# The first sequence's tokens at the head of the queue, rows of weights behind them, and a new timetable for a two-layer kernel

## The chip, the core and the metric

The kernel runs on one core of a Trainium2 chip. Five engines each work through a queue of their own in order: TensorE (PE) multiplies matrices, VectorE (DVE) does elementwise work and scans, ScalarE (ACT) does functions such as exp and SiLU, GpSimd (POOL) gathers, scatters and adds, SyncE (SP) issues transfers (DMA). Semaphores order the engines among each other. The metric is the device time of one execution in microseconds.

## The reference

Eight sequences of 1024 tokens of width 128 go through two layers. Each half of a layer adds its result to x after a layer norm:

```python
x = L0_attn_x                                       # (8, 1024, 128)
x = x + L0_attn(layernorm(x))   # state = state * decay + k v^T, out = q state, per head, then o_w
x = x + L0_ffn(layernorm(x))    # 8 experts (hidden 352), the best 2 of each token: W2(silu(W1 x) * W3 x)
x = x + L1_attn(layernorm(x))   # conv3, silu, selective scan with 16 states, gate, Wout
x = x + L1_ffn(layernorm(x))    # 8 experts (hidden 128), best 2, and two shared experts
```

## The kernel before

Each of the 32 halves (8 sequences, 4 kinds) is a generator that records operations with an engine, what they read and write, and a time wanted (`sched.at`). Nothing is issued at recording. `Schedule.run` then walks through all operations, estimates when each could start, and emits them; the order in which it emits an engine's operations is that engine's queue on the chip. The estimates do not reach the chip: only the order does.

Three things steer the order. `TIMES` has a row for each sequence: a time for the load of its x, and for each half the time of its first, second and last step, with the steps between spaced evenly. An operation with a lower time goes first among those that can start. `START` has the times of loads that belong to no sequence: `START[0]` for `w_rows` (the experts' weights of layer 0 copied in DRAM into one row of 1088 numbers for each expert and partition: W1T, W3T, a block of zeros, three parts of W2T), `START[1]` to `START[4]` for the zeroing of the four buffers `xd` into which tokens are scattered, `START[5]` for `f_rows` (the experts' weights of layer 1). Four numbers set the choice in `run`: `NEAR` (how much later than the earliest possible start an operation may start and still be chosen by its time), `AHEAD` and `STAY` (how far ACT keeps to operations of the function table that it holds before it loads the other), and `TABLE` (the estimate of a load).

```python
soon = max(min(start for start, _ in able), clock[e]) + NEAR
_, start, o = min((o.at, start, o) for start, o in able if start <= soon)
```

The loads of `w_rows`, `xd`, `f_rows` and x are made with `hold=True`, by `load` (L453): they don't start before their time in `run`'s estimate. All plain transfers go out on SP's queue; the constants (L264, L282, L294, L343 to L346) go out on ACT's, ahead of ACT's first computing.

The halves work like this. Layer 0's attention (`l0_attn`): layer norm (`normal`: statistics on DVE L478, Ln and Exp on ACT, scaling on ACT L494), transposes on PE (L508), projections (L462), v written to DRAM (`v_rows`) and read back as eight tiles `kv` in which each head's row is repeated; for each tile a product, a scan (L757) and a product on DVE, and in two groups of four the products with `o_rep` on PE (L647), added to x by DVE. Layer 0's experts (`l0_ffn`): routing on DVE (with the counts on PE, L583 and L584), a scatter of tokens to `xd` by POOL (16 indirect transfers, L813), then 23 blocks of 128 tokens. For each: the weights of its expert fetched (`we`, L870, three buffers), the tokens `xg` loaded and transposed in pairs (L856), the first product on PE (L925), SiLU on ACT, a product on DVE (`h`), the second product on PE (L904, recorded one block late), a scaling on ACT (L879), a store to `yd`; at the end a gather and add by POOL (L832, L421). Layer 1's attention (`l1_attn`): for each of 16 states exp on ACT, two products on PE that spread a row (L462, from `eye3b`), a product, a scan (L1025) and a product on DVE, and an add on POOL. Layer 1's experts (`l1_ffn`) are like layer 0's in pairs of blocks (L1129, L1110), but for the last sequence, where all experts run densely (`l1_ffn_dense`). Five buffers hold x, so up to five sequences are in work.

Of the kernel before, what the change touches and what calls it, by code (L numbers as in the profile page):

```python
# [50 lines left out]

PE, DVE, ACT, POOL, SP = ENGINES = "PE", "DVE", "ACT", "POOL", "SP"
HOP = 0.1
NEAR = 0.000
TABLE = 1.3
AHEAD = 139.9
STAY = 808.88


FREE = "wide", "acc", "row", "tile64", "xg", "xgT", "h", "ysb"  # L60


TIMES = (
    (0.00, (818.90, 1322.01, 2108.68), (3522.25, 4588.46, 4795.69), (4797.48, 4983.83, 4992.58), (5030.92, 5042.54, 5223.89)),
    (67.14, (3166.92, 3983.92, 4510.55), (4699.80, 4856.34, 4927.28), (4997.29, 5212.77, 5286.76), (5404.61, 5424.23, 5749.45)),
    (109.51, (4187.39, 4691.07, 4889.13), (4901.24, 4939.80, 5127.57), (5251.15, 5545.42, 5789.16), (5810.49, 5812.68, 6004.33)),
    (120.45, (4793.10, 4906.69, 4971.56), (5082.33, 5219.46, 5502.99), (5722.81, 6084.57, 6157.33), (6169.97, 6173.73, 6677.38)),
    (236.36, (5055.60, 5281.59, 5442.24), (5660.84, 5668.06, 5941.03), (5949.96, 6234.77, 6774.15), (6878.69, 6968.14, 7691.04)),
    (479.09, (5388.91, 5651.37, 5789.26), (5874.46, 5982.25, 6396.69), (6719.00, 7084.49, 7401.94), (7715.74, 7724.19, 8166.75)),
    (809.61, (5867.01, 6125.06, 6365.51), (6586.67, 6776.94, 7240.89), (7646.86, 8055.63, 8649.36), (8989.08, 9535.91, 10103.79)),  # L70
    (976.52, (6289.32, 6518.36, 6888.36), (7137.22, 7366.30, 7806.48), (8156.41, 9711.12, 9827.21), (9899.41, 10070.31, 10173.34)),
)

START = -2834.48, 135.59, 64.01, 104.85, 731.91, 32.55


class Buf:
# [20 lines left out]
class Schedule:  # L98
# [45 lines left out]
    def run(self):  # L144
# [3 lines left out]
        for _ in range(len(self.ops)):  # L148
            best = None
            for e in ENGINES:  # L150
# [15 lines left out]
                if same:  # L166
# [5 lines left out]
                        or c[1].table == table  # L172
                        or clock[e] - c[0] > STAY
                        or c[1].at[0] + AHEAD < min(same)
                    ]
                soon = max(min(start for start, _ in able), clock[e]) + NEAR
                _, start, o = min((o.at, start, o) for start, o in able if start <= soon)
# [33 lines left out]
def preln_two_layer_kernel(ctx: ExitStack, tc: tile.TileContext, a: dict, out: bass.AP):  # L211
# [239 lines left out]
    def load(out_, in_, kb, r, w, hold=False):  # L451
        op(
            SP, 0.45, lambda: nc.sync.dma_start(out_(), in_()), r, w, land=2.3 + kb / 300.0,  # L453
            hold=hold,
        )
# [229 lines left out]
    w_rows_b, f_rows_b = Buf(None, w_rows), Buf(None, f_rows)  # L685
    sched.at = START[0]
    for j, name in enumerate(("W1T", "W3T")):
# [17 lines left out]
    for i, v in enumerate(xd_b):  # L705
        sched.at = START[1 + i]
        load(
            lambda v=v: v.f.rearrange("(b p) d -> p b d", p=P),
            lambda: zrow.unsqueeze(1).to_broadcast([P, NBLK, XW]), 1483, [], [v], hold=True,
        )  # L710
    sched.at = START[5]
    for j, name in enumerate(("w1T", "w3T", "w2T")):
# [533 lines left out]
```

## Time and profile before

| | us |
|---|---|
| median of 3 runs (2008.73 to 2019.97) | 2010.96 |
| the profiled execution | 2010.04 |
| its span, first to last instruction | 2007.9 |
| DVE busy | 1445.7 (72%) |
| PE busy | 1383.3 (69%) |
| ACT busy, of it 254.0 in 198 loads of a function table | 1000.1 (50%) |
| POOL busy | 891.4 (44%) |

The mean granted TensorE clock was 0.826. A line of the timeline has the start and the length in us, the engine (SPq and ACTq: the sequencer issues a transfer), the line of the kernel, the operation, out<-in, and in brackets how long the engine had been idle and what ended that. A line of the waits has who waited for whom: us in total, times, the longest. A line of the groups ends with busy us, mean ns of one, and the idle time just before.

### The profile page before, as it was taken

Reading aid. Unit: us, or ns where it says so; the run is one execution under the profiler, and the core shown is the slowest. Engines: PE = TensorE matmul, PEld = TensorE weight load, DVE = VectorE, ACT = ScalarE, POOL = GpSimd, SP = SyncE. Lnnn points to the kernel's source line nnn. Section 1 sums busy time; section 2 is a strip of 40 time slices with the busy share of each in tenths; the row PEclk is TensorE's granted clock in tenths of the full one; section 3 lists DMA queues with packets and bytes.
Section 4 is the critical chain, followed back from the end, with each engine's and each line's share of the span. In section 5 each row is a group of like instructions: output and inputs, shape, how many; then the busy total and the mean of one; then the engine's idle time right before and its main releaser. Section 6 shows DMA issues by size and latency. Waiting matters only on the chain. (4 is left out here: it accounts for less than half of the span.)

```text
span 2007.9 us, 24885 instructions
## 1 busy us (share of the span) xinstructions
PE 1383.3 (69%) x7693; PEld 1060.4 (53%) x7693; DVE 1445.7 (72%) x2117; ACT 1000.1 (50%) x1657; POOL 891.4 (44%) x662
## 2 busy tenths in 40 slices
PE   0557787775875678667766686675776788566588
PEld 0335676663554566446655465455665576343364
DVE  0687557767847997699766876679857745789955
ACT  1323443743865475455745447363544576583341
POOL 0003205246135851484643554438635626646613
PEclk9778988877988789769978697786888798796679
DMA  5685668443345458445537463454454566232232
GB/s 161 134 159 157 192 185 232 132 123 112 112 137 156 116 159 203 118 143 144 168 111 200 110 183 121 125 152 126 135 154 143 159 199 190 80 99 59 74 108 58
DMA packets 215740, 282.54 MB, mean 141 GB/s; under 512 B 24248, under 2 KB 173112, under 8 KB 215608
## 3 DMA queue, kind: packets, MB, share of 16 engines
q1 hardware_dynamic: 194504, 247.81, 44.0%
q0 software_dynamic: 15360, 31.61, 5.3%
q10 hardware_dynamic: 5744, 1.54, 0.3%
q8 instruction: 61, 1.00, 0.2%
q14 instruction: 71, 0.58, 0.1%
HBM read 223.62 MB, written 63.15 MB: 143 GB/s over the span
## 5 line engine op out<-in xcount | busy, mean ns | idle before, releaser
L421 POOL TENSOR_TENSOR y<-y,st 128x1024 f32<-128x1024 f32 x120 | 293.1, 2443 | 296.4 <-DVE st L421 257.8
L925 PE MATMUL wide<-xgT,we 128*128 128x128 f32 x2208 | 328.6, 308 | 74.6 <-DVE st L1025 21.7
L832 POOL DMA_INDIRECT tmp<-yd,at x240 | 260.3, 1085 | 260.5 <-issue 59.1
L925 PEld LDWEIGHTS wide<-xgT,we 128*128 128x128 f32 x2208 | 308.1, 221 | 103.6 <-issue 29.4
L1025 DVE TENSOR_TENSOR_SCAN st<-da,wide 128x1024 f32<-128x1024 f32 x128 | 292.4, 2284 | 8.1 <-POOL y L421 0.3
L462 PE MATMUL wide<-term,eye3b 96*128 96x512 bf16 x512 | 181.4, 453 | 128.5 <-DVE st L1025 72.5
L393 ACT ACT_TABLE_LOAD x198 | 254.0, 1283 | 16.1 <-DMA gbias<-in_gate_bias_dram 12.7
L813 POOL DMA_INDIRECT xd<-xw,at x120 | 124.5, 1038 | 222.3 <-DVE at L634 162.7
L904 PE MATMUL acc<-we,h 128*128 128x128 f32 x1104 | 173.4, 298 | 70.4 <-DVE h L421 34.1
L446 ACT ACTIVATE h<-wide 128x384 f32<-128x384 f32 x184 | 89.4, 490 | 256.0 <-PE wide L925 158.6
L879 ACT ACTIVATE ysb<-acc,xg 128x128 f32<-128x128 f32 x345 | 116.7, 363 | 184.2 <-PE acc L904 70.4
L904 PEld LDWEIGHTS acc<-we,h 128*128 128x128 f32 x1104 | 153.6, 208 | 98.2 <-DVE h L421 31.0
L421 DVE TENSOR_TENSOR wide<-dtx,wide 128x1024 f32<-128x1024 f32 x128 | 156.4, 1223 | 58.3 <-remote 43.2
L446 ACT ACTIVATE da<-dt,a_mat 128x1024 f32<-128x1024 f32 x128 | 145.2, 1146 | 101.3 <-DVE st L1025 65.6
L647 PE MATMUL acc<-o_rep,kv 128*128 128x128 f32 x1024 | 150.0, 313 | 50.6 <-DVE kv L421 34.7
L421 DVE TENSOR_TENSOR h<-h,wide 128x384 f32<-128x384 f32 x184 | 99.2, 546 | 108.3 <-ACT h L446 85.4
L647 PEld LDWEIGHTS acc<-o_rep,kv 128*128 128x128 f32 x1024 | 144.4, 227 | 58.6 <-DVE kv L421 37.4
L421 DVE TENSOR_TENSOR st<-st,wide 128x1024 f32<-128x1024 f32 x120 | 146.2, 1218 | 34.9 <-PE wide L462 13.1
L757 DVE TENSOR_TENSOR_SCAN kv<-lam,kv 128x1024 f32<-128x1024 f32 x64 | 152.3, 2380 | 1.4
L462 PEld LDWEIGHTS <-eye3b 96*128 96x128 bf16 x512 | 57.3, 112 | 177.7 <-issue 165.8
L1129 PE MATMUL acc<-xgT,fe 128*128 128x128 f32 x644 | 119.9, 340 | 39.5 <-DMA fe<-f_rows 11.5
L792 POOL COPY tmp<-xw 128x1024 f32<-128x1024 f32 x15 | 19.5, 1297 | 280.4 <-ACT xw L494 208.3
(149 smaller groups left out, 2292.1 us busy)
## 6 DMA issues: line engine op xcount, KB each, us to landing
we<-w_rows SPq DMA_DIRECT2D x184, 544.0 KB
kv<-v_rows SPq DMA_DIRECT2D x64, 512.0 KB
fe<-f_rows SPq DMA_DIRECT2D x169, 192.0 KB
xg<-xd SPq DMA_DIRECT2D x165, 129.0 KB
yd<-ysb SPq DMA_DIRECT2D x165, 128.0 KB
xd<-zrow SPq DMA_DIRECT2D x4, 1483.5 KB
x<-in_x_dram SPq DMA_DIRECT2D x8, 512.0 KB
v_rows<-tmp SPq DMA_DIRECT2D x8, 512.0 KB
```

Of the source, the lines that this page charges most:

```text
L393: nc.scalar.add_instruction(mybir.InstLoadActFuncSet(name=nc.get_next_instruction_name(), act_func_set_id=tables[table], ins=[], outs=[]))
L421: op(eng, us, lambda: e.tensor_tensor(out_(), in0(), in1(), alu), r, w)
L446: op(ACT, act_us(n), lambda: nc.scalar.activation(out_(), in_(), func, **kw), r, w, table)
L462: nc.tensor.matmul(dst.f[:m, ts(s, HALF)], lhsT(), rhs()[:, ts(s, HALF)], start=True, stop=True)
L647: nc.tensor.matmul(v3(po, 4, P)[:, i, :], h.f[:, ts(4 * q + i, P)], w(), start=(j == 0), stop=(j == len(parts) - 1),)
L757: lambda kv=kv: nc.vector.tensor_tensor_scan(kv.f, lam.f, kv.f, 0.0, ALU.mult, ALU.add),
L813: lambda k=k, c=c: nc.gpsimd.indirect_dma_start(out=views[k * NC + c], out_offset=bass.IndirectOffsetOnAxis(ap=v3(at, TOPK, NC)[:, k, c : ...
L832: lambda k=k, c=c, g=g: nc.gpsimd.indirect_dma_start(out=v3(g, NC, P)[:, c, :], out_offset=None, in_=yd[i], in_offset=bass.IndirectOffsetO ...
L904: nc.tensor.matmul(py.f[:, :P], v3(h, 3, P)[:, j, :], we.f[:, c0 : c0 + P], start=(j == 0), stop=(j == 2),)
L925: nc.tensor.matmul(p4[:, m, j, :], we.f[:, c0 : c0 + P], xgT.f[:, ts(i % 2, P)], start=True, stop=True,)
L1025: lambda st=st, da=da, pb=pb: nc.vector.tensor_tensor_scan(st.f, da.f, pb.f, 0.0, ALU.mult, ALU.add),
L1129: nc.tensor.matmul(p13.f[:, ts(n * m + q, P)], w[q].f[:, ts(m, P)], xgT.f[:, ts(q, P)], start=True, stop=True,)
```

## The change

Only numbers change: `NEAR`, `AHEAD`, `STAY`, all of `TIMES` and `START`.

```diff
-NEAR = 0.000
+NEAR = 0.026
 TABLE = 1.3
-AHEAD = 139.9
-STAY = 808.88
+AHEAD = 280.8
+STAY = 739.99
...
 TIMES = (
-    (0.00, (818.90, 1322.01, 2108.68), (3522.25, 4588.46, 4795.69), (4797.48, 4983.83, 4992.58), (5030.92, 5042.54, 5223.89)),
-    (67.14, (3166.92, 3983.92, 4510.55), (4699.80, 4856.34, 4927.28), (4997.29, 5212.77, 5286.76), (5404.61, 5424.23, 5749.45)),
...
+    (0.00, (6.27, 3398.78, 3554.88), (4192.81, 4342.63, 5153.14), (5283.34, 5488.99, 5692.35), (5759.30, 5785.35, 5941.47)),
+    (8.29, (3256.27, 4319.75, 4860.50), (5029.34, 5476.77, 5617.00), (5754.74, 5919.28, 6065.68), (6112.39, 6219.32, 6542.53)),
...
-START = -2834.48, 135.59, 64.01, 104.85, 731.91, 32.55
+START = 63.56, 2.00, 197.96, 464.21, 301.83, 2.00
```

In SP's queue the first sequence's x now stands first, followed by the zeroing of `xd0`, the three copies of `f_rows` and the second sequence's x; the six copies of `w_rows`, which stood first, come after the first 17 transfers. The zeroing of `xd1`, `xd2` and `xd3` comes later in the queue than the first fetches of `we`. The queues of all five engines hold the same operations in another order; ACT's holds 178 loads of a function table at L393 where it held 198.

## The prediction

> **What bounds the kernel now.** I read the page first: is any engine full?
>
> ```profile
> span 2007.9 us, 24885 instructions
> ...
> PE 1383.3 (69%) x7693; PEld 1060.4 (53%) x7693; DVE 1445.7 (72%) x2117; ACT 1000.1 (50%) x1657; POOL 891.4 (44%) x662
> ...
> DVE  0687557767847997699766876679857745789955
> ```
>
> None is. DVE, the busiest, is idle for 562 us (2007.9 - 1445.7). The digits show where: the first slice of 50 us is a 0, the stretch from 1800 us is nearly full, and the middle runs at 6 to 8. So the time is set by who waits for whom in queues whose order is fixed at build time. The waits say on what:
>
> ```profile
> ACT h L446 <- PE wide L925: 158.6, 90, 9.8
> DVE h L421 <- ACT h L446: 116.4, 59, 9.4
> PE wide L462 <- DVE st L1025: 72.5, 40, 9.5
> ```
>
> That is the experts' loop (PE first product, ACT SiLU, DVE product, PE second product) and the scans (DVE frees a PSUM tile for PE). No single hole; many of a few us. The one big hole is the start, read in the timeline of SP, then ACT, then DVE:
>
> ```profile
> 0.75 0.69 SPq L453 DMA_DIRECT2D w_rows<-in_W1T_dram  x1
> 26.04 0.53 SPq L453 DMA_DIRECT2D w_rows<-in_W3T_dram  x1
> ...
> 37.28 2.19 SPq L453 DMA_DIRECT2D x<-in_x_dram  x1
> ...
> 63.89 10.89 SPq L453 DMA_DIRECT2D x<-in_x_dram  x1
> ```
>
> ```profile
> 27.84 1.28 ACT L393 ACT_TABLE_LOAD   x1 [12.66 <-DMA gbias<-in_gate_bias_dram]
> 46.57 0.30 ACT L446 ACTIVATE row<-row,eps 128x8 f32<-128x8 f32 x1 [17.44 <-DVE row L427]
> ...
> 56.92 1.28 ACT L393 ACT_TABLE_LOAD   x1
> 58.22 1.11 ACT L446 ACTIVATE tmp<-wide,cs_b 32x1024 f32<-32x1024 f32 x1
> ```
>
> ```profile
> 44.28 1.65 DVE L478 BATCH_NORM_STATS2 stats<-x 128x6 f32<-128x128 f32 x8 [28.85 <-DMA x<-in_x_dram]
> ...
> 64.47 1.23 DVE L421 TENSOR_TENSOR kv<-kT,kv 128x1024 f32<-128x1024 f32 x1 [17.16 <-ACT lam L446]
> ```
>
> The first tokens are issued behind six copies of weights and land at 44.28. ACT issues its constants until 27.82 whatever SP does, then stands 17.44 us. From its first Ln (46.57) to DVE's first heavy product (64.47) is a chain of 17.9 us that the change leaves alone.
>
> **The change part by part.** The sum is made against the profiled execution, 2010.04 us (span 2007.9 and 2.1 around it); the median of the three runs is 0.9 above, which I leave out as smaller than anything below. Instruction counts per engine stay, but for table loads. Orders are read from the built queues; the numbers in the timetable are priorities, and I take no time from them.
>
> *1, the start.* x of sequence 0 becomes SP's first issue, at about 0.75. In before it landed 7.0 us after its issue with a backlog ahead of it, so it is there before 14. What ends last is then ACT: its constants and the table load end at 29.12 (27.84 + 1.28), so Ln moves from 46.57 to 29.12, a gain of 17.4. Behind x in the queue now stands the zeroing of xd0 (1483.5 KB); in before the W1T copy (1408 KB) stood there, so ACT's constants meet about the same traffic. But the zeroing is in small rows, and the x issued behind the zeroing at 63.15 was held for 10.89 us; if ACT's issues were held as long, only 6.5 of the 17.4 would stay. I take 15 (2.4 off), as W1T is the nearer row: **-15**, bounds -17.4 and -6.5.
>
> *2, the copies of weights, later.* The six w_rows issues now stand in SP's queue behind the first v row of sequence 1. SP's three kv loads before them went out at 92.94 to 94.74, so about 78 to 80 now. The six took 0.69 + 0.53 + 0.57 + 9.42 = 11.2 us of issue. Queued behind them are four kv loads of sequence 1 (DVE's next scans) and x of sequence 2. These kv loads wait for PE to free their buffers anyhow, in before until 118.17, now about 103. The bytes, 4352 KB = 4.46 MB at the 243 GB/s of the stretch 26 to 49, need 18.3 us and end near 98. Cover 23 us against 18.3: **0**; without that cover, up to 11.2 for the issue or 18.3 for the bytes. The three f_rows copies and x of sequence 1 now wait at the front of SP for its DMA semaphores to be released by ACT's constants (W3T did until 26.04); then 1.57 + 0.52 MB at 243 GB/s, 9 us, end before 40, ahead of the first v store (56.93 - 15). Nothing.
>
> The Trainium skill speaks against counting that as free: its page "DMA: Bandwidth & Descriptors", section "Issuing engines are not separate DMA queues", says that DMAs of all issuing engines run on the same 16 DMA engines and interleave. The row at 63.89 (10.89 us of issue against 0.58 for another x at 120.67) agrees that a backlog is felt by the next transfer. By that rule with nothing hidden, 18.3 us come back and the sum below would end at 2015.
>
> *3, zeroing of xd1, xd2, xd3.* In before two of these three, xd1 and xd2, were issued in the first 110 us and only xd3 among the experts' fetches; now all three stand there, each with we fetches (PE's next weights), yd stores and xg loads behind it. The nearest row is xd3 at 772.52: the fetch behind it went out only at 779.04, but PE's second product that frees its buffer ended at 779.0, so the zeroing cost nothing visible. Far end: 10.9 each (the 63.89 row), 22 for the two more. I take **+2**, near the nearest row.
>
> *4, table loads.* ACT's queue holds 178 in the place of 198 (L393).
>
> ```profile
> L393 ACT ACT_TABLE_LOAD x198 | 254.0, 1283 | 16.1 <-DMA gbias<-in_gate_bias_dram 12.7
> ```
>
> 20 x 1.283 = 25.7 us of ACT. How much lies on the path? The chain that ended last reaches back to about 1757; in these 251 us ACT made 19 loads, 24.4 us, of which the chain holds 0.3% of the span, 6.0 us: a quarter. So **-6**, bounds 0 and -25.7. Here the trace and the skill differ: "ScalarE: Activation LUTs", section "What ACT_TABLE_LOAD costs", adds a drain of 1.38 us to each load, 2.66 in all. The load at 56.92 is followed by the next activation at 58.22, 1.30 later, so no such drain shows; by the page this term would be -13 and the sum 1990.
>
> *5, the new order on DVE.* The order decides which waits are covered by a long instruction queued just ahead. I sorted before's DVE instructions by kind and by whether their predecessor in the queue is a long one (a scan, a 128x1024 product, a stats step). The x additions (66) stood idle 0.77 us each behind a long one and 2.20 behind a short one; 28 and 38 of them before, 37 and 29 now: 9 x (0.77 - 2.20) = -12.9. The experts' h products (184): 0.38 and 0.84; 102 and 82 before, 93 and 91 now: 9 x 0.46 = +4.1. Other kinds change by under 4 us each. **-9**; as averages over few cases this could be 0 or twice as much.
>
> *6, the new order on PE.* Between a block's first and second product PE needs other work while ACT and DVE make h: 0.49 + 0.55 us, hops, and often a scan of 2.28 ahead on DVE, some 3 us. I summed PE work queued in between (1.79 us for a first product, 0.94 for a second, 1.8 for a projection's two matmuls and so on, from busy time by line) and added up what each block lacks to 3 us. Layer 0's experts lack 42 us in sum in before and 65 now; layer 1's 34 and 50. Token transposes to first product (need 1.5 us) lack 26 and 36. Together +49 us of PE made to wait. PE holds 4% of the about 12.5% of the span that the chain names, a third: **+15**, bounds 0 and +49.
>
> From about 1720 on, where the last scans fill DVE and the dense experts end the program, both queues hold nearly the same work in the same order: 0.
>
> **Sum:** -15 + 0 + 2 - 6 - 9 + 15 = -13, so 2010 - 13 = **1997 us**. By itself this case spans about 1980 to 2010 (terms 5 and 6 off by a dozen each).
>
> **The rivals.** *A, slower: the tighter experts' loop.* One mechanism: PE reaches the second product before h is there and blocks, and behind it in PE's queue stand the products for the scans, so DVE starves too. Paid in full, and with term 5 not coming true: 2010 + 49 + 2 - 15 - 6 = **2040**. For it: the two longest waits of the page are on this loop. Against: PE is idle 31% anyway, so much of it falls into holes that exist. It decides from about 57% paid on (28 of 49, with terms 1, 4 and 5 as taken), and clearly from 78%.
>
> *B, no change: the start is given back at once.* After sequence 0's routing counts PE has 12.8 us of work queued before the transposes that need the scattered tokens; in before 30.1. The scatter that they wait for took from 147 to 174. So PE blocks 17.3 us earlier, and the 15 saved are waited out there: 2010 + 2 - 6 - 9 + 15 = **2012**. For it: that scatter does not get shorter. Against: DVE has 26.6 us of its own work for that stretch (35.8 before), and work not done there is only moved.
>
> *C, much faster:* table loads sit in the SiLU and exp chains throughout, and all 25.7 count, the start brings 17.4, DVE gains 9, PE loses nothing: 2010 - 52 = **1958**. For it: ACT feeds most waits. Against: ACT is half idle.
>
> **Chances.** Forecast 0.42, A 0.25, B 0.15, C 0.18. About 0.5% (10 us) is what a measurement of this kernel can tell from no change. Faster by more (under 2001): C and 0.30 of the forecast's 0.42, 0.48. Within: 0.12 of the forecast and 0.10 of B, 0.22. Slower: A and 0.05 of B, 0.30. The range, 1958 to 2040, runs from C to A and leaves out the outer halves of both.
>
> **What would show it.** Right: the first slice of DVE no longer 0; Ln near 30 and the first kv product near 49; 178 table loads at 1.28; the last 290 us unchanged. Term 6: the waits "PE acc L904 / PE wide L925 <- DVE h" and "ACT h <- PE wide" longer than before. B: a hole on PE of over 10 us just after the first scatter, and milestones level with before by 300 us. Wrong: an Ln after 40 (constants held by the zeroing), a stall of kv loads near 80 to 100 (copies not hidden), or holes of several us beside each xd zeroing.

## The result, and the profile after

The changed kernel takes 2041.16 us (median of 4 runs, 2037.52 to 2045.2) beside 2009.85 for the kernel before (4 runs): ratio 1.0163, 95% interval 1.0133 to 1.0192. It is 1.6% slower, where 1997 was forecast; the time lies just above the range of 1958 to 2040. The profiled execution took 2037.64 us, with a granted clock of 0.82.

The page of after, its head and DVE's digits:

```profile
span 2035.8 us, 24897 instructions
...
PE 1392.9 (68%) x7693; PEld 1067.5 (52%) x7693; DVE 1445.3 (71%) x2117; ACT 976.6 (48%) x1637; POOL 898.4 (44%) x662
...
DVE  1865647996576988898775785898657435888955
...
L393 ACT ACT_TABLE_LOAD x178 | 228.4, 1283 | 15.9 <-DMA bout<-in_bout_dram 12.8
```

The work is the same, ACT's is 23.5 us less. The first slice is no longer 0. Far behind it, in slices 31 to 34 (1527 to 1730 us), stands "7435" where before has "7745"; the digits hardly show the loss.

The same waits as before the change:

```profile
DVE h L421 <- ACT h L446: 174.3, 73, 11.3
ACT h L446 <- PE wide L925: 173.5, 87, 5.9
PE wide L462 <- DVE st L1025: 54.5, 39, 4.3
```

The first grew by 58 us, the second by 15, the third fell by 18. A sum over the program doesn't say where. For that I lined up DVE's queue of both kernels by the work done, counted in before's durations. When DVE had been given 300, 700, 1000 and 1200 us of work, before stood at 471, 935, 1332 and 1569 us and after at 447, 921, 1314 and 1556: after was 13 to 24 us **ahead**. Not at every mark: at 100 and at 500 us of work the two were level, and at 200 after was 9.5 us behind. At 1250 us of work it was 1631 and 1666: 35 **behind**. In one stretch, from 1556 to 1666 us, after loses 48 us, more than the whole difference. Not all of it stays lost: at 1275 us of work after is 14 us behind, at 1300 it is 22.

The timeline of DVE in that stretch of after (start, length, line, operation, and the idle time before it with what ended it):

```profile
1596.05 2.28 DVE L1025 TENSOR_TENSOR_SCAN st<-da,wide 128x1024 f32<-128x1024 f32 x1
...
1625.53 0.42 DVE L421 TENSOR_TENSOR h<-h,acc 128x256 f32<-128x256 f32 x1 [7.06 <-ACT h L446]
...
1646.05 0.55 DVE L421 TENSOR_TENSOR h<-h,wide 128x384 f32<-128x384 f32 x1 [2.37 <-issue]
1646.52 1.64 DVE L478 BATCH_NORM_STATS2 stats<-x 128x6 f32<-128x128 f32 x8
```

The scan at 1596.05 is the last of sequence 5's layer 1. The statistics at 1646.52 are those of sequence 6's layer 1, which need the combine of sequence 6's experts (16 gathers and two adds on POOL). Between the two DVE has only short h products, each waiting for the chain PE, ACT, DVE. POOL's timeline shows the combine that the statistics need, from its first gather to its last, and its second add:

```profile
1607.42 0.98 POOL L832 DMA_INDIRECT tmp<-yd,at  x1 [5.27 <-DMA xg<-xd]
...
1628.43 0.94 POOL L832 DMA_INDIRECT tmp<-yd,at  x1 [0.30 <-issue]
...
1637.32 2.36 POOL L421 TENSOR_TENSOR x<-x,tmp 128x1024 f32<-128x1024 f32 x1
```

It ends at 1639.68; by the order in which the kernel emits POOL's queue, the gathers behind 1628.43 belong to sequence 4. For the last 7 us the statistics stand behind sequence 7's h products in DVE's queue, and not behind the combine.

In before the same combine runs from 1582.82 to 1614.5, and DVE has scans left for it (before's DVE timeline):

```profile
1591.37 2.29 DVE L1025 TENSOR_TENSOR_SCAN st<-da,wide 128x1024 f32<-128x1024 f32 x1
...
1609.20 2.29 DVE L1025 TENSOR_TENSOR_SCAN st<-da,wide 128x1024 f32<-128x1024 f32 x1
...
1619.84 1.63 DVE L478 BATCH_NORM_STATS2 stats<-x 128x6 f32<-128x128 f32 x8
```

The busy time in the two windows, from sequence 6's last h product in layer 0 to those statistics, first before, then after (columns: window, its length, busy us and instructions of PE, PEld, DVE, ACT and POOL, granted clock, DMA share, GB/s):

```profile
1577.00:1620.00 43.00, 32.36 (x194) 26.69 (x193) 30.60 (x28) 18.90 (x39) 34.14 (x24) 0.83 0.59 176
```

```profile
1601.00:1647.00 46.00, 28.20 (x185) 25.07 (x185) 6.26 (x15) 12.31 (x35) 28.55 (x27) 0.81 0.65 195
```

DVE idles 12.4 us of 43 in before and 39.7 of 46 in after, 34.4 of these until the combine's end. I call the stretch from a sequence's last h product to those statistics a handover, and I call the DVE work queued between its two ends its **cover**. From the orders and before's durations, it is 32 us for sequence 6 in before and 5 in after; of the other seven of layer 0 none has less than 24 in either. The cover is no full measure: sequence 2's is 58 us in after, and DVE idles 25.9 us of 83 in that handover all the same (in before 1.0 of 49.7, with a cover of 51).

The start, in after's timelines of SP, ACT and DVE:

```profile
0.75 0.45 SPq L453 DMA_DIRECT2D x<-in_x_dram  x1
1.48 0.37 SPq L453 DMA_DIRECT2D xd<-zrow  x1
...
84.14 2.88 SPq L453 DMA_DIRECT2D w_rows<-in_W3T_dram  x1
...
92.12 10.52 SPq L453 DMA_DIRECT2D w_rows<-in_W2T_dram  x3
```

```profile
34.01 1.28 ACT L393 ACT_TABLE_LOAD   x1 [12.84 <-DMA bout<-in_bout_dram]
35.30 0.30 ACT L446 ACTIVATE row<-row,eps 128x8 f32<-128x8 f32 x1
```

```profile
5.87 1.07 DVE L478 BATCH_NORM_STATS2 stats<-x 128x6 f32<-128x128 f32 x5 [4.18 <-DMA x<-in_x_dram]
...
55.49 1.22 DVE L421 TENSOR_TENSOR kv<-kT,kv 128x1024 f32<-128x1024 f32 x1
```

x landed at 5.9 and no longer matters. Ln stands at 35.30, not 29, as ACT's issue of constants lasts until 34.0 (27.8 before). The first heavy product is at 55.49, 9.0 us earlier than in before.

### The profile page after: what moved, and what is told of

Read it like the earlier page. It is cut to its first block, busy times and chain, and to the rows that moved or that the text cites. A ratio compares the mean times of both kernels' runs of the same rounds, so it can differ in the third digit from the quotient of the medians.

```text
span 2035.8 us, 24897 instructions
## 1 busy us (share of the span) xinstructions
PE 1392.9 (68%) x7693; PEld 1067.5 (52%) x7693; DVE 1445.3 (71%) x2117; ACT 976.6 (48%) x1637; POOL 898.4 (44%) x662
## 5 line engine op out<-in xcount | busy, mean ns | idle before, releaser
L925 PE MATMUL wide<-xgT,we 128*128 128x128 f32 x2208 | 336.1, 313 | 76.3 <-DVE st L1025 23.3
L925 PEld LDWEIGHTS wide<-xgT,we 128*128 128x128 f32 x2208 | 315.2, 225 | 103.2 <-DVE st L1025 28.5
L462 PE MATMUL wide<-term,eye3b 96*128 96x512 bf16 x512 | 176.7, 444 | 118.5 <-DVE st L1025 52.3
L813 POOL DMA_INDIRECT xd<-xw,at x120 | 129.1, 1076 | 252.7 <-DVE at L634 188.8
L904 PE MATMUL acc<-we,h 128*128 128x128 f32 x1104 | 178.9, 305 | 89.2 <-DVE h L421 51.3
L446 ACT ACTIVATE h<-wide 128x384 f32<-128x384 f32 x184 | 89.2, 489 | 282.7 <-PE wide L925 173.5
L647 PE MATMUL acc<-o_rep,kv 128*128 128x128 f32 x1024 | 136.8, 297 | 50.8 <-DVE kv L421 37.3
L757 DVE TENSOR_TENSOR_SCAN kv<-lam,kv 128x1024 f32<-128x1024 f32 x64 | 162.6, 2541 | 1.4
L647 PEld LDWEIGHTS acc<-o_rep,kv 128*128 128x128 f32 x1024 | 131.5, 211 | 56.5 <-DVE kv L421 39.5
L1129 PE MATMUL acc<-xgT,fe 128*128 128x128 f32 x644 | 118.1, 339 | 48.2 <-ACT xgT L449 27.9
L1129 PEld LDWEIGHTS acc<-xgT,fe 128*128 128x128 f32 x644 | 106.1, 244 | 70.9 <-ACT xgT L449 36.4
```

What stands on the lines that cost most here:

```text
L446: op(ACT, act_us(n), lambda: nc.scalar.activation(out_(), in_(), func, **kw), r, w, table)
L462: nc.tensor.matmul(dst.f[:m, ts(s, HALF)], lhsT(), rhs()[:, ts(s, HALF)], start=True, stop=True)
L647: nc.tensor.matmul(v3(po, 4, P)[:, i, :], h.f[:, ts(4 * q + i, P)], w(), start=(j == 0), stop=(j == len(parts) - 1),)
L757: lambda kv=kv: nc.vector.tensor_tensor_scan(kv.f, lam.f, kv.f, 0.0, ALU.mult, ALU.add),
L813: lambda k=k, c=c: nc.gpsimd.indirect_dma_start(out=views[k * NC + c], out_offset=bass.IndirectOffsetOnAxis(ap=v3(at, TOPK, NC)[:, k, c : ...
L904: nc.tensor.matmul(py.f[:, :P], v3(h, 3, P)[:, j, :], we.f[:, c0 : c0 + P], start=(j == 0), stop=(j == 2),)
```

## The experiments

The runs fell on four chips. On one, by its times that of the first comparison, before took 2008 to 2010 us; on the three others, one for e5 to e8, one for e13 to e16 and one for e17 and e18, it took 1841 to 1850. So each ratio is against before on the same chip. In the cuts of code, square brackets tell in words what a list holds, and dots stand for what is left out. Where an order is given by hand, `run` follows a written list in the place of its choice.

**First four: which part of the change.** *e1*, the front alone, in before's order:

```diff
-  [6 copies of w_rows] [all else, x of sequence 0 after them]
+  [x of sequence 0] [before's order up to sequence 1's first kv load] [6 copies of w_rows] [the rest]
```

> Before's order in every queue, written out as a list, with two moves only: the first sequence's x goes to the head of SP's queue, and the six w_rows copies go behind the first kv load of sequence 1. If the start is a gain by itself (theory): about 12 us faster than before, near 1998, since the changed kernel's first kv product came 9 us earlier and its DVE had done 50 us of work 12 us earlier. If the start is given back at the first scatter (rival): within 3 us of before.

2006.64 us, ratio 1.0002 (0.9972 to 1.0032): nothing that can be measured, as the rival had it. Its DVE timeline shows both sides:

```profile
44.34 1.23 DVE L421 TENSOR_TENSOR kv<-kT,kv 128x1024 f32<-128x1024 f32 x1 [16.71 <-DMA kv<-v_rows]
...
119.95 1.64 DVE L478 BATCH_NORM_STATS2 stats<-x 128x6 f32<-128x128 f32 x8 [18.29 <-DMA x<-in_x_dram]
```

The first heavy product comes 20.1 us earlier than before's 64.47. Then DVE waits 18.29 us for sequence 2's x, which stands in SP's queue behind the copies (3.03 in before). At 50 us of DVE work it is 20 us ahead of before, at 100 only 3.

*e2*, after's order with the front undone:

```diff
-  [x of sequence 0] ... [6 copies of w_rows behind 17 transfers] ...
+  [6 copies of w_rows] [the rest in after's order]
```

> The changed kernel's order in every queue, with the six w_rows copies put back at the head of SP's queue, ahead of x. Theory (the start's gain lasts to the end): about 12 us slower than the changed kernel, near 2053. Rival (given back): within 3 us of 2041.

2051.45, ratio 1.0231 (1.018 to 1.0281), near the forecast: 10 us (2051.45 - 2041.16) of the front's gain are kept in after's order, or 6 beside e9, which is after run again (2045.88). The intervals of e2 and e9 overlap; in the profiled executions e2 is 9 to 14 us behind after at every mark.

*e3* and *e4*, one order first, the other for what is left:

```diff
+  ORDER = first[:cut] + [op for op in second if op not in first[:cut]]   # cut at 1000 us of DVE work
```

> The changed kernel's order until its DVE has been given 1000 us of work (about 1314 us into its span), and then all that is left in before's order. At this point the two orders have done the same operations but for 43 of 5773. Theory (the whole loss is made by the order of the last third): 1314 + (2010 - 1332) = 1992 us, faster than both. Rival (the new order is worse throughout, by less cover in the experts' loop, and the places where it shows are chance): about halfway between the kernels, 2020 to 2030.

> The converse: before's order until DVE has been given 1000 us of work (about 1332 us), and then the changed kernel's order. Theory: 1332 + (2038 - 1314) = 2056 us, slower than both. Rival: halfway, 2020 to 2030.

e3 took 1995.8, ratio 0.9941 (0.9918 to 0.9964), below both kernels; e4 2063.29, ratio 1.0287 (1.0235 to 1.0338). So the loss is made behind the cut, near 1320 us, and on this chip the first two thirds of the change gain 12 us. e4's window from 1622 shows the idle DVE of after, with 5.84 us busy of 48:

```profile
1622.00:1670.00 48.00, 27.51 (x185) 23.96 (x185) 5.84 (x14) 12.11 (x34) 30.27 (x29) 0.86 0.62 188
```

**Four on where in the late order.** Cuts at 1150 and 850 with the diff of e3 (*e5*, *e8*), and sequence 6's layer 0 set to the other kernel's place (*e6* in after, *e7* in before):

```diff
+  ORDER = after's, with sequence 6's layer-0 operations put where before has them (by DVE work ahead)   # e6; e7 the converse
```

> After's order until DVE has been given 1150 us of work (near 1490 us of the run), before's order for what is left. After's profile falls behind only between 1556 and 1666 us. Theory 1 (the cause is earlier: after puts layer 0's experts of sequence 6 about 60 us of DVE work later, from 967 to 1027, so that at 1600 us more of its blocks are left, with nothing long to lie beside them): at 1150 that has been done, so the loss is in this kernel too: 2020 to 2040. Rival (the order of the last 400 us itself, where the time is seen to be lost, is the cause): it is replaced here, so about the 1996 of the kernel cut at 1000.

> After's order; only the operations of sequence 6 in layer 0 (attention and experts) are moved to the place they have in before, by the DVE work queued ahead of them (experts from 968 instead of 1027); all other operations keep after's order among themselves. Theory 1 (sequence 6's experts are late): most of the 45 us between after and the kernel cut at 1000 comes back: 1996 to 2012. Rival (it is not that sequence, but the rest of the late order): 2030 to 2045.

> The converse: before's order; only sequence 6's operations in layer 0 are moved to the place they have in after (experts from 1027 instead of 967). Theory 1: the loss appears by itself: 2030 to 2055. Rival: about 2009, as before.

> After's order until DVE has been given 850 us of work (near 1120 us of the run), then before's. The cut at 1000 took 1996, 12 to 14 us less than before. If that gain is made at the start and in the first 900 us (after is 12, then 24 us ahead at 50 and 300 us of DVE work): about 1996 to 2000. If it is made between 850 and 1000: about 2008, as before.

These fell on a faster chip (before 1841.51). e5: 1897.13, ratio 1.0303 (1.0243 to 1.0363); e6: 1943.87, 1.0552 (1.0495 to 1.061); e7: 1988.84, 1.0783 (1.0718 to 1.0848); e8: 1856.06, 1.0075 (1.0048 to 1.0103). e6 gives my first theory, "sequence 6 is late", no support: with that sequence put earlier the kernel is far slower. And e5 is slow by something that neither kernel has. Its SP and PE timelines:

```profile
1377.87 0.34 SPq L870 DMA_DIRECT2D fe<-f_rows  x1
1410.28 0.95 SPq L453 DMA_DIRECT2D out_dram<-x  x2
```

```profile
1417.83 1.44 PE L925 MATMUL wide<-xgT,we 128*128 128x128 f32 x5 [32.31 <-DMA we<-w_rows]
```

Behind the cut SP's queue comes at once to sequence 3's output store, and POOL's queue to that sequence's combine, but on POOL it stands behind ten scatters of sequence 4 that after's part had begun. The store waits until 1410, all fetches of weights behind it wait, and PE stands 32.31 us. In e7 PE stands 28.5 us before 1621. A splice through unlike queues makes holes of its own, so I take nothing from e5 to e7 about the change. e8 has no such hole; that it is 0.75% slower than before, and not faster like e3, I can't place without a profile of before on that chip.

**Four on one sequence, with orders that the kernel's own builder makes from changed times.** *e9* is after once more, *e12* e3 once more. *e10* and *e11* change after's timetable:

```diff
-  sequence 3: ..., (7113.73, 7120.54, 8128.85)
+  sequence 3: ..., (7113.73, 7120.54, 7700.00)                                            # e10
-  sequence 6: (6721.43, 6725.94, 7464.91), (7740.22, 8020.67, 8156.44), ...
+  sequence 6: (6687.41, 6849.54, 7109.01), (7345.65, 7549.24, 8045.67), ...              # e11
```

> After itself, to stand beside the next three on one chip. On the chip of the first comparison it took 1.6% more than before. If the loss lies in the order alone, the ratio is the same anywhere: about 1.016. If it lies in the stretches of that chip's trace in which PE, ACT and DVE all stand still while POOL issues indirect transfers (after has some 26 us more of them than before from 1473 us on), it is smaller where these are missing: 0.995 to 1.005.

> After with one number of the timetable changed: sequence 3's last layer is due to end at 7700 instead of 8128.85. The builder orders it anew from about 915 us of DVE work on: sequence 3's layer-1 combine comes 100 us of DVE work earlier (1066, before the dispatch of sequence 6's tokens, instead of 1166, after the dispatch of sequence 4's). Theory 2 (that combine, whose 16 transfers and output store stand in POOL's and SP's queues in front of what sequences 6 and 7 wait for, is what the late order loses by): at least half of the gap between after and the cut at 1000 comes back, 20 us or more below after. Rival: within 10 us of after.

> After with sequence 6's times for layer 0 put back to those of before, on after's scale; the builder makes a whole new order from it (sequence 6's experts start after 935 us of DVE work, as against 1029 in after and 970 in before, and their combine comes before that of sequence 3). Theory 1 (sequence 6's layer 0 is late): 20 us or more below after. Rival (the loss is not in that sequence): within 10 us of after, or slower.

> The kernel cut at 1000 us of DVE work once more (after's order first, then before's), on the same chip as after itself. On the first chip it took 0.994 of before and 45 us less than after. If that holds for the order and not for the chip: again 0.99 to 1.00 of before and 35 to 55 us below after.

On the first chip (before 2010.08): e9 2045.88, 1.016 (1.0101 to 1.0218); e12 1999.07, 0.9946 (0.9919 to 0.9972); both repeat. e10 2069.24, 1.0296 (1.0244 to 1.0349), and e11 2080.44, 1.0362 (1.03 to 1.0424): both theories missed, on the wrong side. What the traces of the four say of the combine of sequence 6: e12 has DVE busy 30.59 of 43 us there, like before; e10 5.64 of 45, for it leaves that cover at 5; e11 has a cover of 39, but sequence 3's combine and others now stand close together on POOL, and the handover takes 75 us, with DVE idle for 39 of them.

```profile
1562.00:1605.00 43.00, 33.28 (x192) 26.70 (x191) 30.59 (x28) 19.38 (x39) 33.96 (x24) 0.79 0.58 175
```

```profile
1517.00:1592.00 75.00, 39.97 (x157) 27.93 (x156) 35.86 (x58) 23.98 (x41) 52.16 (x50) 0.62 0.33 96
```

**Four on the standstills.** On the first chip there are standstills, stretches in which PE, ACT and DVE all stand still while POOL issues indirect transfers; behind 1320 us they sum to 40 us in after and 15 in before. Theory 3 was that these are the loss.

```diff
-  nc.gpsimd.indirect_dma_start(...)                      # 8 for each group
+  nc.gpsimd.dma_start(...)  (the first of 8);  6 x nc.gpsimd.tensor_copy(scr, scr)  (each of 8)
```

> Before's order, with its indirect transfers taken out: each group of eight is replaced by one plain transfer of the same rows to or from fixed places, and POOL is kept busy by small copies in the place of each of the eight (so the tokens reach other rows than they should, and the output is not the reference's). It gives the base for the next two; by the 60 to 75 us of standstill that lie in the bursts of before's profile, 1900 to 1960 if POOL's bursts last as long as before.

> The same with after's order (again the tokens reach other rows). Theory 3 (the late order loses because a handover that is late during a burst of indirect transfers finds nothing else queued on the three engines): without the indirect transfers the loss is gone, and it stands within -15 to +8 us of the kernel with before's order. Rival (the late order is longer by itself, whatever POOL does): 25 to 40 us above it.

> The same with the order cut at 1000 (again the tokens reach other rows). Theory 3: level with the kernel of after's order, within 15 us. Rival: 35 to 50 us below it, as with the indirect transfers.

> After itself on the same chip. Where the standstills in the bursts are as on the first chip: 1.016 of before. Where they are missing: by theory 3, 0.99 to 1.005; by its rival, 1.012 to 1.025.

2183.87, 2197.79 and 2218.2 us: inconclusive. The small copies took longer than what they replaced (POOL busy 1451.2 us in e13), POOL became the bound, and the three say only that an order's worth hangs on POOL's durations. e16, after on a faster chip, did tell: 1877.58 beside 1850.28, ratio 1.0159 (1.0107 to 1.0211), the same as on the first chip, with one standstill of 2 us behind 1320. So the standstills are not the whole loss, as theory 3 had it. That they are a part of it on the first chip stays open: after stands 45 to 47 us above the cut at 1000 there, with standstills behind 1320 of 40 us against 15 in e12, while e16 stands only 16 us (by the ratios to before) to 21 us (1877.58 - 1856.06) above e8. And e8 is itself 0.75% above before, so on the faster chips, by these ratios, about half of after's 1.6% is there ahead of the late order.

e16 and e8 are after and a cut of after on two of the faster chips. Up to 1225 us of DVE work (1471 us) their DVE milestones stay within 10 us and are 2.4 apart at its end; at 1250 they are 27.9 apart, at 1275 8.1, and 16 to 18 at the end. The windows of the combine of sequence 6, e8 and then e16:

```profile
1454.00:1491.00 37.00, 29.35 (x190) 24.34 (x190) 30.18 (x27) 18.77 (x39) 29.42 (x23) 0.90 0.65 204
```

```profile
1485.00:1521.00 36.00, 26.77 (x203) 23.37 (x203) 5.43 (x11) 13.02 (x36) 21.92 (x21) 1.00 0.88 269
```

Idle 6.8 us of 37, and 30.6 of 36. That made theory 4: the uncovered handover.

**Two on the cover**, again by the timetable alone, e17 in after and e18 in before:

```diff
-  sequence 4: ..., (7985.75, 8071.37, 8206.30)
+  sequence 4: ..., (7965.75, 8051.37, 8186.30)                    # e17
-  sequence 6: ..., (7740.22, 8020.67, 8156.44), ...
+  sequence 6: ..., (7740.22, 7950.67, 8086.44), ...               # e17
-  sequence 6: ..., (6586.67, 6776.94, 7240.89), ...
+  sequence 6: ..., (6586.67, 6896.94, 7360.89), ...               # e18
```

> After with sequence 6's experts due 70 units earlier (two numbers) and sequence 4's layer-1 experts 20 earlier (three numbers); the builder's order is the same up to operation 3892 of 5773. DVE then has 28 us of work queued between sequence 6's last h product in layer 0 and the layer norm that waits for the combine, in the place of 5 in after; every other combine and dispatch of tokens keeps 27 us or more (24 and 26 in two early ones, as in after). Theory 4 (a combine takes about 30 us, and what DVE lacks to that is waited out): 23 us of the 45 to 48 come back at least, more if the standstills around it go too: 1.005 of before or less, 15 to 45 us below after. Rival (the late order is slow throughout): 1.012 to 1.025 of before, as after.

> The converse: before with sequence 6's experts due 120 units later (two numbers). The cover of its combine falls from 32 us to 10, that of the other handovers stays at 27 or more where it was (dispatch of sequence 6 63, of sequence 7 49). Theory 4: 20 us of DVE's time are waited out: 1.007 to 1.02 of before. Rival: 0.997 to 1.004 of before.

On a faster chip (before 1846.93) e18 took 1881.2, ratio 1.0191 (1.0164 to 1.0218): before loses 34 us when the cover falls from 32 to 10, somewhat more than the 20 expected. Lined up with e8, which has before's order in this part, e18 loses 23 us from 1225 to 1275 us of DVE work, where the handover lies, and 15 more up to 1400, behind it. Its two numbers also move blocks of sequences 5 and 7 by some 10 us of DVE work, so not all of the 34 need be the cover's. Its window, DVE idle 29.0 us of 39:

```profile
1461.00:1500.00 39.00, 31.26 (x247) 28.09 (x246) 10.00 (x18) 14.67 (x40) 23.27 (x19) 1.00 0.90 275
```

e17 took 1927.67, ratio 1.0445 (1.0419 to 1.0471), a clear miss. The handover itself was mended (the first window), but not the time (second window, and PE's timeline):

```profile
1445.00:1484.00 39.00, 25.99 (x135) 19.67 (x133) 26.84 (x25) 19.80 (x39) 29.05 (x25) 0.81 0.66 190
1494.00:1528.00 34.00, 0.00 (x0) 0.00 (x0) 2.19 (x3) 4.24 (x9) 27.07 (x27) 0.50 0.24 71
```

```profile
1528.18 1.04 PE L856 MATMUL acc<-ident,xg 128*128 128x128 f32 x3 [34.29 <-DMA xg<-xd]
```

POOL now does the combine of sequence 6, that of sequence 3 and the scatter of sequence 7 right behind one another; PE, with all other sequences' blocks done, stands 34.29 us for sequence 7's tokens. The cover that I counted leaves out what POOL has queued in front of a handover's transfers.

**What is settled and what is open.** Shown: on the first chip the loss is made by the order behind 1320 us (e3, e4, e12); in after, e4, e9, e10 and e16, which have a cover of 5 there, DVE idles 31 to 43 us in sequence 6's handover, and 7 to 12 in before, e12 and e8, which have 32; a change of before that takes the cover down to 10 costs 34 us, 23 of them around that handover (e18). Not shown: that the cover is the whole cause, and that giving it back to after, and nothing else, returns the loss, since e17 moved the hole to the next handover. The idle DVE time is 27 us more in after (39.7 - 12.4), at most that much of the 45 to 47 between after and the cut at 1000. The rest, and what the standstills add on the first chip, I can't assign.

## Why the prediction was wrong

*The start (term 1, -15).* Mechanism right, size off: 9.0 at the first heavy product. ACT's constants do depend on what SP issues: they were held, as the lower bound had it, and Ln stands at 35.30 in the place of 29.12. And the chain from Ln to the first heavy product, counted as unchanged, took 20.2 us, not 17.9. In e1, where another transfer stood behind x, the gain was 20.1. In after it did not last: at 100 us of DVE work the two kernels were level.

*The copies (term 2, 0).* They issue for 19.3 us (83.31 to 102.64), not 11.2. In e1 they cost 15.3 us (18.29 - 3.03) by way of sequence 2's x; the cover of 23 us that I counted was that of the kv loads, and this x stood behind them too. The page of the Trainium skill that the prediction set against its zero ("DMA: Bandwidth & Descriptors", section "Issuing engines are not separate DMA queues") says that transfers of all issuing engines run on the same 16 DMA engines and interleave. e1 agrees that the copies are not free, but it does not show this sharing by itself: that x was also issued only at 104.71, behind the copies in the same queue. In after's order the front still kept 6 to 10 us (e2).

*Zeroings (term 3, +2).* The next issue on SP came 11.0, 11.6 and 3.1 us behind those of after's xd1, xd3 and xd2. No run isolates them. After was still ahead at 1200 us of work, so they did not decide.

*Table loads (term 4, -6).* 178, as counted, 25.6 us less of ACT. The cut at 1000 has 176 and gains 11 to 12 us in all; the share of this is not separated.

*The order (terms 5 and 6, -9 and +15).* This is the step that failed. Both price the order by averages over kinds of instructions and over the whole program, +6 together. On the first chip the order behind 1320 us alone cost 45 to 47. Term 6's wait did grow, here in before and then after:

```profile
PE acc L904 <- DVE h L421: 34.1, 32, 3.3
PE acc L904 <- DVE h L421: 51.3, 30, 10.2
```

But until 1320 us it is 30.3 in before and 28.9 in after, and in e3 it is 27.2 in all: the growth is local to the late order, and not spread over the experts' blocks. The sum "ACT h <- PE wide" does not even tell a good order from a bad one: e3, the fastest on that chip, has 180.0, more than after's 173.5. What showed instead was a loss at one place, sequence 6's combine with 5 us of cover, where DVE idles 27 us more than in before. I had made the right kind of count for one handover only, the first scatter in rival B. Made for all of them from the same two orders, it gives 32 and 5 here and would have put about 25 us on the loss side; that is said in hindsight, and sequence 2's handover shows that the count can miss.

*The last 290 us (0).* Nearly right: from 22 us behind at 1300 us of DVE work to 28 at the end. The loss lies just ahead of that stretch.

*Rivals.* A named 2040, which is what came, but by chance, for the mechanism was another: it spread 49 us over all experts' blocks, while e3 runs two thirds of the tighter loop and gains. One sign of B did come, as the start's gain was gone by 300 us, but not its hole of over 10 us on PE (the longest between the first scatter and 250 us is 9.0). Its kind of mechanism, a handover that finds too little queued work, came at another place. The sum of -13 agrees with what the first two thirds of the change brought on the first chip (-12 in e3); as single terms were off, that is no proof of them.

## What to carry to other kernels

Where queues are in order and several streams are interleaved, list every handover (scatter, gather) and sum for each the work of other streams queued between its two ends on the engine that waits, and the work queued in front of it on the engine that does it. A cover far below the time that the handover takes, 5 us against some 40 here, is the first place to look at, which no average over the program shows; a large cover is no proof that nothing is lost. Place a loss by lining up two traces by work done, at many marks, before looking at waits. An order spliced from two good orders, or mended at one place, can stall elsewhere by more than it gains: e17 cut the idle DVE time of one handover from 31 to 12 us and made a hole of 34 us at another.

## What was not expected of the hardware

The same kernel took 2008 to 2010 us on one chip and 1841 to 1850 on three others. Between e3 on the first and e8 on one of the others, whose orders differ in part, the busy times are nearly the same (DVE 1453.4 us and 1450.0), with a granted clock of 0.827 and 0.852. Over the 1043 us in which e3 and e8 have the same order, e3 falls 79 us behind, nearly all in steps of 2 to 10 us while POOL issues a burst of scatters or gathers: an activation or a DVE operation starts some us after the last matmul that it waits for has ended by the profile (in e3 the SiLU at 1592.69 needs matmuls that ended at 1586.30). Such standstills of all three engines over 1.5 us sum to 50.4 us behind 100 us in e3 and 3.8 in e8. What holds the engines there stays open.
